# Moving the requests of three loads within a pipelined graph-attention and expert kernel

## The chip, the cores and the metric

The kernel runs on one core of one Trainium2 chip. A core has TensorE (matrix products, PE in the profile, with its weight loads as PEld), VectorE (DVE), ScalarE (ACT), GpSimd (POOL), and SyncE (SP), which here only requests transfers. Sixteen DMA engines move the data; transfers are requested by SyncE and ScalarE, or by GpSimd where rows are gathered by index. The metric is the device time of one execution in microseconds, the median of the runs.

## The reference

128 graphs of 128 nodes with 1024 features each pass through graph attention with 16 heads and then through a mixture of two of eight low-rank experts. Cut to what matters:

```python
h  = layernorm(x)                                  # x: (128 graphs, 128 nodes, 1024)
Wh = h @ W                                         # W: 1024 x 1024, 16 heads of 64
e  = leaky_relu(Wh . a1 + Wh . a2, 0.2)            # one score per node and head
att = softmax(where(adj == 0, -9e15, e)) * adj
x  = x + elu(att @ Wh)
y  = layernorm(x)
g  = softmax(top2(y[:, 0, :] @ router.T))          # a gate per graph from its first node
x  = x + (y + sum_e g_e * (y @ down_e.T) @ up_e.T) # 8 experts of rank 16, two are chosen
```

## The kernel before

The main loop takes two graphs in a step q, 64 steps and two more for the tail. The projection of two graphs is done in seven products (a Strassen-like scheme on 2 x 2 blocks: a11, a12, a21, a22 of x transposed and their sums s1 to s4). Each step has eight gaps: the tasks of gap k are issued ahead of product k+1 of that step, so each engine does its tasks in this order. The experts are handled for a group of four graphs, in a pair of steps: in the first (part 0) the router chooses two experts of each graph and GpSimd requests their weights at the end; in the second (part 1, a "fetching step") these weights arrive, the down product runs in gap 4 and the up product in gaps 5 and 6.

```python
def load_x(q):                                  # x for the sum; six buffers
    for i in (2 * q, 2 * q + 1):
        X[i] = work.tile([P, D], F32, tag="x", name="xn", bufs=6)
        nc.sync.dma_start(X[i], x[i])

def load_rows(q):                               # x for the statistics; two buffers
    for i in (2 * q, 2 * q + 1):
        ROWS[i] = work.tile([P, D], F32, tag="rows", name="rows")
        nc.sync.dma_start(ROWS[i], x[i])

def load_xt(q):                                 # x transposed, for the projection; two buffers
    XT[q] = work.tile([P, 2, KC, P], F32, tag="xt", name="xt")
    for t in range(2):
        nc.sync.dma_start(XT[q][:, t], x_t[2 * q + t])

def stats(i, mv):                               # VectorE, called by first_stats(i)
    for h in range(NH):
        nc.vector.bn_stats(st[:, h, :], ROWS[i][:, h * HALF:(h + 1) * HALF])
    nc.vector.bn_aggr(mv[:, i % 2], st)

def pair_sums(q):                               # GpSimd: s1 to s4 of the next step's projection
    nc.gpsimd.tensor_tensor(s1, a21, a22, ALU.add)
    nc.gpsimd.tensor_tensor(s2, s1, a11, ALU.subtract)
    nc.gpsimd.tensor_tensor(s3, a11, a21, ALU.subtract)     # s3 is written over a21
    nc.gpsimd.tensor_tensor(s4, a12, s2, ALU.subtract)

def turn(i):                                    # x after attention, transposed by a DMA
    nc.scalar.copy(halves, X[i].bitcast(U16).rearrange("p (d s) -> p s d", s=2))
    nc.sync.dma_start(TT[i], halves.rearrange("p s d -> p (s d)"), transpose=True)

def first_row(i):                               # SyncE; waits for update(i) on VectorE
    nc.sync.dma_start(GRP[g]["rows"][t:t + 1], X[i][0:1])

def fetch(g):                                   # end of part 0
    # ... indices on VectorE ...
    for j in range(G * TOP):                    # eight requests for the down weights
        nc.gpsimd.indirect_dma_start(out=..., in_=table, in_offset=...)
    for t in range(G):                          # four for the up weights, 512 KB each
        nc.gpsimd.indirect_dma_start(out=..., in_=up_table, in_offset=...)

def ffn_down(g):                                # pd on TensorE (64 matmuls in the profile), then
    # ... 8 chunks x 4 graphs into one accumulator pd ...
    nc.scalar.mul(whole[:, 0], pd[:, 0:P], st["gate"])              # line 845
    nc.vector.scalar_tensor_tensor(whole[:, 1], ...)                # line 846
    for t in range(G):
        for s in range(G):                      # line 850: the casts, half on each engine
            (nc.vector.tensor_copy if s // 2 else nc.scalar.copy)(
                dn[s * GR:(s + 1) * GR, t], whole[t * GR:(t + 1) * GR, s // 2])

def ffn_up(g, t):                               # pu: two accumulators a graph, from a pool of four
    for h, pu in enumerate(st["pu", t]):
        nc.tensor.matmul(pu, st["dn"][:, t], st["up", t][:, h * HALF:(h + 1) * HALF], ...)

def add_up(g, t):                               # VectorE: frees the two accumulators
    for h, pu in enumerate(st.pop(("pu", t))):
        nc.vector.scalar_tensor_tensor(y[:, cols], pu, st["rstd"][:, t:t + 1], y[:, cols], ...)
    nc.sync.dma_start(out[g * G + t], y)
```

The main loop, cut to the tasks that are spoken of:

```python
for q in range(NQ + 2):
    g, part = divmod(q - 2, 2)
    ffn = 0 <= g < NG
    # ...
    gaps[1] += [(attend, i), (update, i)]             # i = 2q - 2; first_row(i) too
    gaps[2] += [(turn, i), (update, i + 1), (squares, i)]   # and first_row(i + 1)
    gaps[3].append((turn, i + 1))
    gaps[4].append((rejoin, i))                       # ScalarE takes the transposed tile
    gaps[5].append((rejoin, i + 1))
    # ...
    if q + 1 < NQ:
        if q:
            gaps[3].append((first_stats, 2 * q + 2))
        gaps[4 if q else 5].append((pair_sums, q + 1))
        if q:
            gaps[4].append((first_stats, 2 * q + 3))
    # ...
    elif ffn and part:
        gaps[0].append((weigh, g))
        gaps[4].insert(0, (ffn_down, g))
        gaps[5][0:0] = [(ffn_up, g, 0), (ffn_up, g, 1), (add_up, g, 0), (add_up, g, 1)]
        gaps[6] += [(ffn_up, g, 2), (ffn_up, g, 3), (add_up, g, 2), (add_up, g, 3)]
    # ...
    if q + 1 < NQ:
        load_xt(q + 1)                                # ahead of all gaps of this step
        load_rows(q + 1)
    if 0 < q < NQ:
        gaps[6].insert(0, (load_x, q))
    # ...
    for gap in gaps:
        for f, *args in gap:
            f(*args)
        next(products, None)                          # the next of the seven products
```

Of the kernel before, what the change touches and what calls it, by code (L numbers as in the profile page):

```python
# [26 lines left out]
def adj_ffn_kernel(  # L27
# [32 lines left out]
    NG, _, G, _ = adj.shape  # L60
# [45 lines left out]
    def load_rows(q):  # L106
# [5 lines that stand above are left out]
    def load_xt(q):  # L112
# [3 lines that stand above are left out]
# [830 lines left out]
    def keep(name, f, *of):  # L946

        def task():
            got[name] = f(*(got.get(o, o) for o in of))
        return (task,)  # L950

    def prepare(gaps):

        gaps[0] += [(place_a,), (pair_sums, 0)]
        gaps[1] += [keep("part 0", partial_means, 0)]
        gaps[2] += [(keep_c11,), keep("part 1", partial_means, 1),
                    (center_block, 0, B11), (combine, T3, B22, T1, ALU.subtract),
                    (combine, T2, T3, B11, ALU.add)]
        gaps[3] += [(center_block, 1, B22), (combine, T1, B22, T2, ALU.subtract),
                    (sums_of, 0), keep("less", less), keep("", correct, "less", 1),  # L960
                    (load_adj, 0)]
        gaps[4] += [(score_rows, 0, 0), keep("", correct, "less", 2),
                    (center_block, 0, B21), (combine, NT4, B21, T2, ALU.subtract),
                    (sums_of, 1), (squares_of, 0), (high, 0, 0)]
        gaps[5] += [(score_rows, 0, 1), (score_rows, 1, 0), (score_rows, 1, 1), (load_experts,),
                    keep("turned", center_rows)]
        gaps[6] += [keep("", turn_rows, "turned"), (score_columns,), (low, 0, 0)]

        gaps[7] += [keep("", turn_scores, "scores")]
# [4 lines left out]
    for q in range(NQ + 2):  # L974
        gaps = [[] for _ in range(8)]
        if q == 0:
            prepare(gaps)
        g, part = divmod(q - 2, 2)
        ffn = 0 <= g < NG
        if ffn and not part:  # L980
            gaps[6] += [(logits, g), (choose, g)]
            if g < NG - 1:
                gaps[6].append((fetch, g))
        if q < NQ:
            gaps[6] += [(high, q, 3), (high, q, 1)]
            gaps[7].append((high, q, 2))
        if ffn and not part:
            gaps[6].append((ratio, g))
            if g == NG - 1:
                gaps[6].append((weigh, g))  # L990
        if 0 < q <= NQ:
            i = 2 * q - 2
            gaps[0].append((attention_weights, q - 1))
            if q > 1:
                gaps[1] += [(join, i - 2), (join, i - 1)]
            gaps[1] += [(attend, i), (update, i)]
            gaps[2].append((attend, i + 1))
            if q < NQ:
                gaps[2] += [(turn, i), (update, i + 1), (squares, i)]
                gaps[3].append((turn, i + 1))  # L1000
                gaps[4 if ffn and part else 3].append((squares, i + 1))
                gaps[5 if ffn and part else 3].append((second_stats, q - 1))
                gaps[4].append((rejoin, i))
                gaps[5].append((rejoin, i + 1))
            else:
                gaps[2] += [(squares, i), (update, i + 1), (turn_at_end, i),
                            (keep_turned, i)]
                gaps[3] += [(squares, i + 1), (turned_parts, NG - 1, False),
                            (turn_at_end, i + 1), (stay_busy, 1, ident), (turned_parts, NG - 1, True),
                            (keep_turned, i + 1), (second_stats, q - 1)]  # L1010
            if q == NQ:
                gaps[7] += [(join, i), (join, i + 1)]
            if i < B - G:
                gaps[1].append((first_row, i))
                gaps[2].append((first_row, i + 1))
        if q + 1 < NQ:
            if q:
                gaps[3].append((first_stats, 2 * q + 2))
            gaps[4 if q else 5].append((pair_sums, q + 1))
            if q:  # L1020
                gaps[4].append((first_stats, 2 * q + 3))
        if ffn and not part:
            if g < NG - 1:
                gaps[3].append((spread_rows, g))
                gaps[4].append((row_parts, g))
        if q == NQ - 1:
            gaps[1].append((load_all,))
            gaps[3].append((load_router,))
            gaps[5].append((order_all,))
        if q == NQ:  # L1030
            gaps[2].insert(1, (down_dense, NG - 1, 0, 2, range(0, 4)))
            gaps[3][0:0] = [(down_dense, NG - 1, 0, 2, range(4, 8)), (stay_busy, 2, ident)]
        if ffn and part and g == NG - 1:
            gaps[0] += [(gates_dense, g), (up_dense, g)]
# [5 lines that stand above are left out]
        if q % 2 == 0 and q < NQ:  # L1040
            gaps[5].append((group_adj, q // 2))
            if q // 2 + 1 < NG:
                gaps[5].append((load_adj, q // 2 + 1))
        if q < NQ:
            if q:
                gaps[3].insert(0, (low, q, 0))
            gaps[6 if q else 7] += [(low, q, 3), (low, q, 1)]

        if q + 1 < NQ:
            load_xt(q + 1)  # L1050
            load_rows(q + 1)
        if 0 < q < NQ:
            gaps[6].insert(0, (load_x, q))
        if q == 0:
            gaps[7] += [(sums_of, 2), (sums_of, 3), (load_up,)]
        if q == 1:
            gaps[0].append((squares_of, 1))
            gaps[1].append((up_parts,))
            gaps[5] += [keep("tables", table_parts), keep("router", router_sums)]
            gaps[7].append(keep("", experts, "tables", "router"))  # L1060
        products = project(q) if q < NQ else iter(())
# [3 lines that stand above are left out]
            next(products, None)  # L1065
# [46 lines left out]
```

## Time and profile before

| What | Before |
|---|---|
| time, median of 3 runs (lowest to highest) | 1982.6 us (1980.53 to 1983.49) |
| span of the profiled execution | 1980.3 us |
| granted TensorE clock, mean | 0.997 |
| mean rate of all DMA | 226 GB/s, 446.87 MB |
| SyncE's queue (q1) | 353.70 MB, 58.9% of the DMA engines' time |
| GpSimd's queue (q0) | 89.68 MB, 14.5% |
| xt, x for statistics, x for the sum | 127, 126 and 128 requests of 512 KB |
| gathered down and up weights | 248 and 124 requests |

A row of a waits view reads "who waited <- for what: us in total, times, longest us". "issue" means that the profile shows nothing that was waited for. A row of a timeline reads: start in us, duration in us, engine, line, operation, output<-inputs, and how many instructions; in brackets the idle time ahead of it and what ended it. Ends of matmuls are modelled, so the distance from one start to the next start tells more than a duration. A row of a windows view holds the stretch, its length, the busy us and the number of instructions on TensorE, its weight loads, VectorE, ScalarE and GpSimd, and then the granted clock, the DMA engines' mean busy share and GB/s. Names: pw is the accumulator of the projection, ph of the attention, pd of the down product, pu of the up product; xn is x for the sum, rows is x for the statistics (and, with 4 KB, the first rows), tt is a tile transposed by DMA.

### The profile page before, as it was taken

How to read it: one execution, taken by the hardware profiler on the slowest of the kernel's cores; microseconds unless marked ns; L12 is line 12 of the kernel's file. 1: busy time of each engine (PE TensorE's matmuls, PEld its weight loads, DVE VectorE, ACT ScalarE, POOL GpSimd, SP SyncE). 2: the span in 40 equal slices, each digit the busy share in tenths (PEclk: the TensorE clock that was granted, in tenths of full speed). 3: DMA queues.
4: the chain of work that ended last, by engine and by line, in shares of the span. 5: the costliest groups of instructions: out<-in, count | busy, mean ns of one | idle time of the engine just before them, and what ended most of it. 6: DMA issues, size and time to landing. Idle time of an engine off the chain costs nothing.

```text
span 1980.3 us, 30167 instructions
## 1 busy us (share of the span) xinstructions
PE 1907.6 (96%) x10182; PEld 1590.9 (80%) x10182; DVE 1689.8 (85%) x3802; ACT 1294.6 (65%) x1564; POOL 944.1 (48%) x1260
## 2 busy tenths in 40 slices
PE   9999999999999999999999999999999999999997
PEld 6878887788888788888888888888888888777885
DVE  6888898888898888888888988888888889888897
ACT  3766666766577666667666676676676666665665
POOL 3346544455444455444555444554444654436541
PEclk9999999999999999999999999999999999999999
DMA  8688767877777767677777777777778676778755
GB/s 323 185 236 200 242 216 224 238 221 213 246 236 202 255 209 237 219 229 235 243 206 241 225 220 240 211 226 236 235 212 255 200 245 218 220 240 204 231 186 166
DMA packets 381058, 446.87 MB, mean 226 GB/s; under 512 B 282732, under 2 KB 284908, under 8 KB 380392
## 3 DMA queue, kind: packets, MB, share of 16 engines
q1 hardware_dynamic: 345320, 353.70, 58.9%
q0 software_dynamic: 30400, 89.68, 14.5%
q10 hardware_dynamic: 5184, 1.57, 0.3%
q8 instruction: 81, 1.33, 0.3%
q14 instruction: 73, 0.60, 0.1%
HBM read 309.58 MB, written 69.22 MB: 191 GB/s over the span
## 4 chain that ended last, share of the span: by engine, by line
PE 86%; DVE 5%; issue 3%; DMA 3%; POOL 2%; ACT 1%; another core or an unknown queue 0%; SPq 0%; DVEq 0%; ACTq 0%
PE pw L480 73%; PE ph L594 5%; PE pd L836 4%; PE pu L858 3%; DMA up<-up_table,at_up 2%; POOL down L820 1%; DVE xn L867 1%; DMA w_sb<-in_w 1%; DVE wh L485 1%; POOL up L826 0%; DVE parts L550 0%; PE pu L922 0%; DVE hp L604 0%; DVE xn L618 0%
## 5 line engine op out<-in xcount | busy, mean ns | idle before, releaser
L480 PE MATMUL pw<-w_sb,xt 128*128 128x260 f32 (+1 forms) x4080 | 935.5, 385 | 0.5 <-DMA w_sb<-in_w 0.5
L480 PEld LDWEIGHTS pw<-w_sb,xt 128*128 128x128 f32 x4080 | 771.7, 190 | 125.5 <-issue 7.0
L480 PE MATMUL pw<-w_sb,s 128*128 128x260 f32 (+1 forms) x3072 | 704.9, 382 | 0.6 <-DVE wh L485 0.6
L480 PEld LDWEIGHTS pw<-w_sb,s 128*128 128x128 f32 x3072 | 582.8, 190 | 95.7 <-DVE wh L485 2.3
L664 ACT COPY y_t<-tt 128x2048 uint16<-128x2048 uint16 x126 | 310.4, 2492 | 54.5 <-DMA tt<-halves 54.3
L638 POOL TENSOR_SCALAR rstd<-acc 128x2 f32<-128x2 f32 x64 | 12.3, 193 | 693.9 <-ACT unread L626 681.6
L658 ACT COPY halves<-xn 128x2048 uint16<-128x2048 uint16 x126 | 239.9, 1904 | 88.5 <-DVE xn L618 73.1
L820 POOL DMA_INDIRECT down<-table,at_down x248 | 260.5, 1050 | 77.8 <-issue 65.8
L546 ACT ACTIVATE parts<-wh,rstd 128x512 fp32r<-128x512 f32 x192 | 136.9, 719 | 227.9 <-DVE wh L485 227.9
L604 DVE TENSOR_TENSOR hp<-ph,att 128x512 f32<-128x512 f32 x256 | 166.0, 684 | 25.9 <-remote 10.2
L618 DVE SCALAR_TENSOR_TENSOR xn<-ex,xn 128x1024 f32<-128x1024 f32 x128 | 156.8, 1225 | 34.7 <-ACT ex L611 24.6
L611 ACT ACTIVATE ex<-hp 128x1024 f32<-128x1024 f32 x128 | 135.1, 1055 | 69.9 <-DVE hp L604 43.5
L867 DVE SCALAR_TENSOR_TENSOR xn<-pu,rstd,xn 128x512 f32<-128x512 f32 x248 | 168.5, 741 | 1.0 <-PE pu L858 1.0
L594 PE MATMUL ph<-parts,adj_f 128*128 128x512 f32 x512 | 164.7, 443 | 1.7 <-ACT parts L546 0.9
L485 DVE TENSOR_TENSOR wh<-pw,p 128x520 f32<-128x520 f32 (+1 forms) x192 | 131.7, 686 | 35.8 <-PE pw L480 20.4
L612 DVE SCALAR_TENSOR_TENSOR xn<-hp,xn 128x1024 f32<-128x1024 f32 x128 | 156.8, 1225 | 4.4
L377 DVE BATCH_NORM_STATS2 stats<-rows 128x6 f32<-128x512 f32 x248 | 158.6, 681 | 0.4
L826 POOL DMA_INDIRECT up<-up_table,at_up x124 | 135.1, 1089 | 37.8 <-issue 37.2
L684 ACT ACTIVATE xn<-xn,off,mul 128x1024 f32<-128x1024 f32 x128 | 151.8, 1235 | 0.0
L626 ACT ACTIVATE unread<-xn,acc 128x1024 fp8e4<-128x1024 f32 x126 | 143.9, 1142 | 3.3 <-DVE acc L620 2.5
L550 DVE SCALAR_TENSOR_TENSOR parts<-wh,rstd,parts 128x512 fp32r<-128x512 f32 x192 | 137.7, 743 | 6.9 <-ACT parts L546 6.8
L836 PE MATMUL pd<-y_t,down 128*32 128x128 f32 x1984 | 84.2, 277 | 42.0 <-issue 41.9
(187 smaller groups left out, 1890.1 us busy)
## 6 DMA issues: line engine op xcount, KB each, us to landing
xn<-in_x SPq DMA_DIRECT2D x128, 512.0 KB
xt<-in_x_t SPq DMA_DIRECT2D x127, 512.0 KB
rows<-in_x SPq DMA_DIRECT2D x126, 512.0 KB
out_y<-xn SPq DMA_DIRECT2D x124, 512.0 KB
adj_f<-in_adj_t POOLq DMA_DIRECT2D x32, 256.0 KB
adj_i<-in_adj SPq DMA_DIRECT2D x32, 256.0 KB
down<-table,at_down POOLq DMA_INDIRECT x248
w_sb<-in_w SPq DMA_DIRECT2D x3, 1040.0 KB
```

Of the source, the lines that this page charges most:

```text
L377: nc.vector.bn_stats(st[:, h, :], ROWS[i][:, h * HALF:(h + 1) * HALF])
L480: nc.tensor.matmul(dst[:, j, cols], lhs[:, k, :], w_sb[:, rhs, k, j, cols], start=(first and k == 0), stop=(k == KH - 1), skip_group_check ...
L594: nc.tensor.matmul(PH[i][h], GRP[g]["adj_f"][:, t, :], PARTS[q][:, s, NH * (i % 2) + h], start=(s == 0), stop=(s == 1))
L604: nc.vector.tensor_tensor(hp[:, h * HALF:(h + 1) * HALF].rearrange("p (h f) -> p h f", f=F), ph.rearrange("p (h f) -> p h f", f=F), att[:, ...
L612: nc.vector.scalar_tensor_tensor(xt, hp, 0.0, xt, op0=ALU.max, op1=ALU.add)
L618: nc.vector.scalar_tensor_tensor(xt, ex, 1.0, xt, op0=ALU.min, op1=ALU.add, accum_out=acc[:, 0])
L658: nc.scalar.copy(halves, X[i].bitcast(U16).rearrange("p (d s) -> p s d", s=2))
L664: nc.scalar.copy(y_of(i).bitcast(U16).rearrange("p k (n s) -> p s k n", s=2), TT.pop(i).rearrange("p (s k) n -> p s k n", s=2))
L684: nc.scalar.activation(X[i], X[i], AF.Identity, bias=GRP[g]["off"][:, t:t + 1], scale=GRP[g]["mul"][:, t:t + 1])
L820: nc.gpsimd.indirect_dma_start(out=st["down"][:, j * R:(j + 1) * R].rearrange("p r k -> p (r k)"), out_offset=None, in_=table, in_offset=b ...
L836: nc.tensor.matmul(pd[t * GR:(t + 1) * GR, 0:P], st["down"][:, t * GR:(t + 1) * GR, k], st["y_t"][:, k, t * P:(t + 1) * P], start=(k == 0) ...
L867: nc.vector.scalar_tensor_tensor(y[:, cols], pu, st["rstd"][:, t:t + 1], y[:, cols], op0=ALU.mult, op1=ALU.add)
```

## The change

In a fetching step, xt and x for statistics of the next step are requested at the head of gap 3 and no longer at the step's start, and what uses them moves too: the two first statistics go from gaps 3 and 4 to gaps 4 and 5, and the pair sums from the end of gap 4 to gap 5, behind the first two graphs of the up product. In the other steps x for the sum is requested at the head of gap 3 and no longer of gap 6. It is meant to keep the time in which the chosen experts' weights are gathered free of other large loads. No operation is added or taken away.

```diff
--- before.py
+++ after.py
@@ -977,6 +977,7 @@
             prepare(gaps)
         g, part = divmod(q - 2, 2)
         ffn = 0 <= g < NG
+        fetching = ffn and part and g < NG - 1
         if ffn and not part:
             gaps[6] += [(logits, g), (choose, g)]
             if g < NG - 1:
@@ -1014,11 +1015,14 @@
                 gaps[1].append((first_row, i))
                 gaps[2].append((first_row, i + 1))
         if q + 1 < NQ:
+
+            late = int(fetching)
             if q:
-                gaps[3].append((first_stats, 2 * q + 2))
-            gaps[4 if q else 5].append((pair_sums, q + 1))
+                gaps[3 + late].append((first_stats, 2 * q + 2))
+            at = gaps[4 + late if q else 5]
+            at.insert(0 if late else len(at), (pair_sums, q + 1))
             if q:
-                gaps[4].append((first_stats, 2 * q + 3))
+                gaps[4 + late].append((first_stats, 2 * q + 3))
         if ffn and not part:
             if g < NG - 1:
                 gaps[3].append((spread_rows, g))
@@ -1047,10 +1051,9 @@
             gaps[6 if q else 7] += [(low, q, 3), (low, q, 1)]
 
         if q + 1 < NQ:
-            load_xt(q + 1)
-            load_rows(q + 1)
+            gaps[3 if fetching else 0][0:0] = [(load_xt, q + 1), (load_rows, q + 1)]
         if 0 < q < NQ:
-            gaps[6].insert(0, (load_x, q))
+            gaps[6 if fetching else 3].insert(0, (load_x, q))
         if q == 0:
             gaps[7] += [(sums_of, 2), (sums_of, 3), (load_up,)]
         if q == 1:
```

## The prediction

> **What bounds the kernel now.** I read the page first (busy shares, then the chain that ended last), then TensorE's waits, then the timeline of one weight-fetching step on all engines, then DMA activity in short windows.
>
> ```profile
> PE 1907.6 (96%) x10182; PEld 1590.9 (80%) x10182; DVE 1689.8 (85%) x3802; ACT 1294.6 (65%) x1564; POOL 944.1 (48%) x1260
> PE pw L480 73%; PE ph L594 5%; PE pd L836 4%; PE pu L858 3%; DMA up<-up_table,at_up 2%; POOL down L820 1%; DVE xn L867 1%; DMA w_sb<-in_w 1%; DVE wh L485 1%; POOL up L826 0%; DVE parts L550 0%; PE pu L922 0%; DVE hp L604 0%; DVE xn L618 0%
> ```
>
> TensorE is the bound: 1907.6 of 1980.3 us, and 73% of the chain is the projection itself. The change removes no matmul, so only idle or slowed TensorE time can be won. TensorE's waits say where that is:
>
> ```profile
> PE pd L836 <- issue: 41.9, 57, 1.9
> PE pu L858 <- DMA up<-up_table,at_up: 6.3, 3, 3.2
> PE pu L858 <- issue: 5.2, 25, 0.2
> ```
>
> All of it lies in the 31 steps that fetch weights: the down product (pd) and the up product (pu). Everything else on TensorE between two such steps is rigid: from the last pu of one to the first pd of the next I read 46.1 us in 26 of the 30 intervals. A usual fetching step in TensorE's timeline:
>
> ```profile
> 1324.82 0.44 PE L836 MATMUL pd<-y_t,down 128*32 128x128 f32 x4
> 1326.30 0.38 PE L836 MATMUL pd<-y_t,down 128*32 128x128 f32 x2 [1.03 <-issue]
> 1327.02 1.91 PE L836 MATMUL pd<-y_t,down 128*32 128x128 f32 x58 [0.34 <-issue]
> 1328.86 3.77 PE L480 MATMUL pw<-w_sb,xt 128*128 128x260 f32 x16
> 1332.63 1.18 PE L858 MATMUL pu<-up,dn 128*128 128x512 f32 x4
> 1333.65 3.67 PE L480 MATMUL pw<-w_sb,s 128*128 128x260 f32 x16
> 1336.97 0.98 PE L858 MATMUL pu<-up,dn 128*128 128x512 f32 x2
> 1338.15 1.11 PE L858 MATMUL pu<-up,dn 128*128 128x512 f32 x2 [0.21 <-issue]
> ```
>
> Two losses are to be seen, by starts. (a) pd takes 1328.86-1324.82 = 4.04 us with 1.03+0.34 us idle. (b) The second four pu take 1339.10 (the next product's start) -1336.97 = 2.13 us where the first four took 1.02: 1.11 us lost. Loss (b) is VectorE's doing; the weight loads of pu wait 20.8 us in 55 waits for its additions (xn, line 867):
>
> ```profile
> 1330.62 0.34 DVE L846 SCALAR_TENSOR_TENSOR dn<-pd,gate,dn 128x128 fp32r<-128x128 f32 x1
> 1330.99 2.98 DVE L850 CAST dn<-dn 32x128 fp32r<-32x128 f32 x8
> 1333.98 1.29 DVE L377 BATCH_NORM_STATS2 stats<-rows 128x6 f32<-128x512 f32 x2
> 1335.31 0.21 DVE L378 BATCH_NORM_AGGREGATE mv<-stats 128x2 f32<-128x12 f32 x1
> 1335.43 0.65 DVE L485 TENSOR_TENSOR wh<-pw,wh 128x520 f32<-128x520 f32 x1
> 1335.99 2.71 DVE L867 SCALAR_TENSOR_TENSOR xn<-pu,rstd,xn 128x512 f32<-128x512 f32 x4
> ```
>
> The additions that free the accumulators start at 1335.99 although their products ended near 1333.8; casts and statistics stand ahead of them. The eight casts take 2.98 us where eight medians of 222 ns make 1.8: one is held up to 1.3 us. Last, the DMA share and GB/s over this step:
>
> ```profile
> 1309.00:1317.00 8.00, 8.00 (x38) 6.87 (x37) 7.43 (x26) 4.24 (x6) 6.02 (x7) 1.00 0.88 334
> 1317.00:1322.00 5.00, 5.00 (x24) 4.29 (x23) 3.83 (x7) 2.45 (x2) 3.93 (x4) 1.00 0.29 68
> 1326.00:1331.00 5.00, 4.36 (x70) 3.68 (x70) 2.98 (x7) 3.75 (x8) 3.60 (x3) 1.00 0.79 295
> 1334.00:1338.00 4.00, 3.94 (x18) 2.91 (x16) 3.96 (x8) 4.00 (x2) 2.06 (x6) 1.00 0.00 0
> ```
>
> xt and x for statistics run in the first window, the gathered down weights trickle in the second, the up weights run in the third, and in the last nothing runs.
>
> **What the Trainium skill says.** "SBUF — State Buffer" lets VectorE casts in a two-port mode and GpSimd exclude each other for a whole instruction. The trace agrees: the long cast lies under GpSimd's pair sums (1.26 to 1.32 us each, 1327.32 to 1332.45). "DMA: Bandwidth & Descriptors", section "Queues, rings and completion order", says that one ring's descriptors start in order and that each DMA engine alternates between rings packet by packet, so xt on the sync queue and up weights on GpSimd's should share. No step before has large loads on both for long, so the even share below is an estimate. Section "Specifications" gives 435 GB/s as ceiling; full windows here show 406 to 418.
>
> **The change part by part.** Nothing is added or removed; three things move.
>
> 1. In 30 or 31 steps, four requests (xt twice, x for statistics twice, 512 KB each, 2.1 MB) leave the step's start (1309.07) for the head of gap 3. On the sync queue that is behind the request of the first rows at 1324.88: not three products but 16 us later, since that request waits for VectorE. Issue is 0.4 us each: 1325.1 to 1327. What this frees is the window 1309 to 1317. What was there with it is the gathered down weights, but their eight requests are paced by GpSimd (1.3 us each, the last 1318.83 to 1319.86), after that window. So I expect no earlier last down weight. The pd idle ends within 0.3 us of 7.0 us after GpSimd's last down request in all 31 steps, also in the last one, which has no xt to load (0.86 us idle against 1.35 on average). I book pd at 0 to -0.3 us per step, i.e. about -5 us in all.
>
> 2. The new load: transposed halves hold the sync queue until about 1325.5, and the time from request to first bytes in the step's start is about 1.7 us (requested 1309.07, traffic from 1310.8). So xt starts near 1327, when up weights still have some 1.2 MB to come (they end at 1330 at about 400 GB/s). Shared evenly at 205 GB/s each, up ends about 5.9 us later, 1332.9, before its last use at 1338. In that time 1.2 MB of mine are in: xt (1.05 MB, done near 1332.1) and 0.15 MB of the first x. The other 0.37 MB at 410 GB/s take 0.9 us: the first x is there near 1333.8, the second near 1335. The turned second tile follows and ends near 1338 where it ended at 1334; ScalarE takes it 1.7 us later than the 1336 of before, and the attention which needs that chain is at 1346.
>
> 3. VectorE in gaps 4 and 5. The first statistics move from before pd's casts to behind them, the second from before the additions of graphs 0 and 1 to behind them. With the pair sums now waiting for xt (1332), the casts run free in 1.8 us. New order: casts 1330.4 to 1332.3; statistics when x is there, t_r; 1.5 us of statistics, 0.6 us for the projection's sum, additions from t_r+2.0. Before: 1335.99. So t_r below 1334.0 is a gain and above it a loss, one for one on TensorE; the gain stops at the 1.1 us of loss (b). My t_r, with 0.2 us of landing, is 1334.0: break-even. Per us of error: 31 us over the kernel.
>
> 4. In about four of the 31 steps the second transpose is requested early, runs mixed with the up weights and makes both crawl; pu then waits 0.6 to 3.2 us (the 6.3 us row) and intervals after two of them are 1.5 us longer. Now 2 MB of xt and x stand between in the same ring, so I book -8 us.
>
> 5. x for the sum comes three gaps sooner in the other steps. Its buffers were freed a step earlier, so no wait; it delays the second transpose there by about 1 MB / 410 = 2.5 us of traffic less the idle it fills, perhaps 1 us, which ScalarE's later waits (0.9 and 1.9 us) absorb. 0 us.
>
> Sum: -5 (pd) + 0 (additions) - 8 (early transposes) + 5 for waits on late x that come unevenly = -8: 1982.6 - 8, about 1975.
>
> **The rivals.** *Full relief:* up weights yield to the sync queue, x is there by 1332.9, additions start 1.1 us sooner: 31 x 1.1 = 34, with the 13 above 1935 to 1940. For it: 4 us of idle DMA after 1334 show room; against: the up weights fill the queue to 1330. *Late x:* transposes are slow when mixed with other traffic (fetching step at 1808 us: pu waited for up until 1823.57), so x comes 1.5 us later, VectorE blocks in gap 4 with the additions behind it: +46, about 2025. For it: everything is now pushed into 1322 to 1335. *The fetch really was in the way:* the pd idle is caused by xt's traffic and goes: -42, about 1940. Against: it ends 7 us after the last request even where no xt was loaded.
>
> **Range and chances.** t_r has an error of about 1.2 us either way, so about 35 us, capped on the good side by 1.1 us. Range 1940 to 2012. Over 2% faster (below 1943) needs full relief or the pd idle gone: 0.12. Over 2% slower (above 2022) needs x over 1.4 us late: 0.10. Within: 0.78.
>
> **What would show it.** Right: pd idle near 40 us still on the page, casts of dn on VectorE at 222 ns with no long one, the second statistics behind four additions, the wait for up weights gone, DMA busy in the former empty 1334 to 1338. Wrong: VectorE's statistics waiting for rows for more than 2 us per step (late x), pd idle falling by more than half, the second four pu at 1.1 us (full relief), or the interval of 46.1 us growing.

## The result, and the profile after

The changed kernel takes 2074.3 us (median of 4 runs, 2070.9 to 2083.4) where the kernel before takes 1982.3 us (4 runs): a ratio of 1.047 with a 95% interval of 1.043 to 1.051. It is slower by 92 us. Predicted were 1975 us, in a range of 1940 to 2012.

The two lines of the page that answer to those of before, the busy time of each engine and the chain that ended last by line:

```profile
PE 1957.8 (95%) x10182; PEld 1621.7 (78%) x10182; DVE 1645.4 (80%) x3802; ACT 1299.2 (63%) x1564; POOL 941.4 (45%) x1260
DMA rows<-in_x 13%; PE pw L480 8%; DMA first_row<-rows 6%; DVE wh L485 5%; DVE hp L604 5%; DVE xn L618 5%; DVE parts L550 5%; DVE xn L867 5%; DVE xn L612 4%; SPq L660 4%; DMA out_y<-xn 3%; DMA rows<-xn 2%; ACT ex L611 2%; DVE stats L377 2%; DVE prod L713 1%
```

The same 10182 matmuls keep TensorE busy 50 us longer, which points to a lower clock (0.981 on the mean against 0.997), and the chain has left TensorE: it was 73% projection before and is now x for statistics (13%), first rows (6%) and VectorE. The view of all waits names the same two loads. Neither load's row was of any size before (none for x; first rows 0.6 us, once):

```profile
ACT y_t L664 <- DMA tt<-halves: 158.5, 62, 5.1
...
DVE stats L377 <- DMA rows<-in_x: 96.5, 30, 5.3
...
PE pd L836 <- issue: 50.3, 102, 1.3
DVE prod L713 <- DMA first_row<-rows: 45.4, 31, 3.7
...
PE pu L858 <- issue: 34.8, 50, 2.7
```

The down product's idle went from 41.9 to 50.3 us, the up product's "issue" wait from 5.2 to 34.8, and its 6.3 us of waiting for up weights are gone. The fetching step that the prediction showed at 1324.82 lies at 1387.54 here. TensorE's timeline of it:

```profile
1387.54 0.54 PE L836 MATMUL pd<-y_t,down 128*32 128x128 f32 x5
1388.65 0.32 PE L836 MATMUL pd<-y_t,down 128*32 128x128 f32 x1 [0.57 <-issue]
1389.37 0.27 PE L836 MATMUL pd<-y_t,down 128*32 128x128 f32 x1 [0.39 <-issue]
1390.09 1.80 PE L836 MATMUL pd<-y_t,down 128*32 128x128 f32 x57 [0.46 <-issue]
1391.86 3.75 PE L480 MATMUL pw<-w_sb,xt 128*128 128x260 f32 x16
1395.25 1.28 PE L858 MATMUL pu<-up,dn 128*128 128x512 f32 x4
1396.37 3.67 PE L480 MATMUL pw<-w_sb,s 128*128 128x260 f32 x16
1400.95 1.11 PE L858 MATMUL pu<-up,dn 128*128 128x512 f32 x2 [0.91 <-issue]
```

pd now takes 4.32 us from its start to the next product's start (4.04 before), and the second four pu start 4.58 us after their product instead of 3.32. The requests on the sync queue and VectorE's work in this step say why:

```profile
1384.11 3.50 SPq L660 DMA_TRANSPOSE tt<-halves  x1
1387.71 0.38 SPq L692 DMA_DIRECT2D rows<-xn  x1
1388.19 0.84 SPq L115 DMA_DIRECT2D xt<-in_x_t  x2
1389.08 1.28 SPq L110 DMA_DIRECT2D rows<-in_x  x2
```

```profile
1393.47 1.89 DVE L850 CAST dn<-dn 32x128 fp32r<-32x128 f32 x8
1398.10 1.29 DVE L377 BATCH_NORM_STATS2 stats<-rows 128x6 f32<-128x512 f32 x2 [2.74 <-DMA rows<-in_x]
1399.42 0.21 DVE L378 BATCH_NORM_AGGREGATE mv<-stats 128x2 f32<-128x12 f32 x1
1399.54 0.65 DVE L485 TENSOR_TENSOR wh<-pw,wh 128x520 f32<-128x520 f32 x1
1400.10 2.72 DVE L867 SCALAR_TENSOR_TENSOR xn<-pu,rstd,xn 128x512 f32<-128x512 f32 x4
```

The casts run free in 1.9 us, VectorE is ready for the statistics at 1395.4, and x lands only at 1398.1. The additions that free pu's accumulators stand behind it and TensorE waits for them.

**Where the 92 us are.** I cut each of the 30 periods between two down products at starts in TensorE's timeline and took means, in us. The projection's products bear the kernel's own numbers: "product 7" is the one between pd and pu, "product 3" the one between the two halves of pu; "rest" is everything from the last pu to the next pd.

| kernel | pd | product 7 | first four pu | product 3 | second four pu | rest | period |
|---|---|---|---|---|---|---|---|
| before | 4.01 | 3.66 | 1.03 | 3.31 | 2.32 | 46.26 | 60.59 |
| after | 5.09 | 3.56 | 1.12 | 4.61 | 2.30 | 46.80 | 63.49 |

The period grew by 2.90 us, which over 31 is 90 of the 92 us: pd 1.08, product 3 with the wait behind it 1.30, the rest 0.54. Most of the last is a matter of the clock. In the 10 of the 30 intervals that hold a stretch at half clock the rest takes 47.7 us, in the other 20 46.35. A windows view of the stretch after pu's wait in the step above (columns as in the prediction: length, busy times, then clock, DMA share, GB/s) shows what makes the 10:

```profile
1399.90:1403.30 3.40, 2.00 (x6) 0.94 (x6) 3.40 (x6) 1.89 (x1) 3.14 (x5) 1.00 0.55 174
1403.30:1406.70 3.40, 3.40 (x11) 2.67 (x10) 3.37 (x7) 1.92 (x3) 1.41 (x5) 0.56 0.77 283
1406.70:1410.00 3.30, 3.30 (x16) 2.83 (x15) 3.20 (x9) 0.58 (x1) 0.00 (x0) 0.94 0.50 128
```

After a stretch with 1.4 us of idle TensorE, 3.4 us follow at about half clock, in which 11 matmuls pass instead of 16. The down product has the same: in 20 steps it took 4.73 us to its last matmul's end (4.08 before), in the other 10, whose matmuls took some 417 ns where 273 is usual, 5.96. Over the whole run the mean clock is 0.981 against 0.997: (1-0.981) x 2069 - (1-0.997) x 1980 = 39.3 - 5.9 = 33 us of full-speed TensorE time, at most, were lost to the clock alone.

### The profile page after: what moved, and what is told of

Same layout as the page of the kernel before. It is cut to its first block, busy times and chain, and to the rows that moved or that the text cites. A ratio compares the mean times of both kernels' runs of the same rounds, so it can differ in the third digit from the quotient of the medians.

```text
span 2069.1 us, 30197 instructions
## 1 busy us (share of the span) xinstructions
PE 1957.8 (95%) x10182; PEld 1621.7 (78%) x10182; DVE 1645.4 (80%) x3802; ACT 1299.2 (63%) x1564; POOL 941.4 (45%) x1260
## 4 chain that ended last, share of the span: by engine, by line
DVE 47%; DMA 25%; PE 9%; issue 7%; ACT 6%; SPq 5%; DVEq 0%; another core or an unknown queue 0%; ACTq 0%; POOL 0%; POOLq 0%
DMA rows<-in_x 13%; PE pw L480 8%; DMA first_row<-rows 6%; DVE wh L485 5%; DVE hp L604 5%; DVE xn L618 5%; DVE parts L550 5%; DVE xn L867 5%; DVE xn L612 4%; SPq L660 4%; DMA out_y<-xn 3%; DMA rows<-xn 2%; ACT ex L611 2%; DVE stats L377 2%; DVE prod L713 1%
## 5 line engine op out<-in xcount | busy, mean ns | idle before, releaser
L480 PE MATMUL pw<-w_sb,xt 128*128 128x260 f32 (+1 forms) x4080 | 950.4, 389 | 2.1 <-issue 0.9
L480 PEld LDWEIGHTS pw<-w_sb,xt 128*128 128x128 f32 x4080 | 783.7, 194 | 134.6 <-issue 11.5
L664 ACT COPY y_t<-tt 128x2048 uint16<-128x2048 uint16 x126 | 314.9, 2500 | 158.7 <-DMA tt<-halves 158.5
L377 DVE BATCH_NORM_STATS2 stats<-rows 128x6 f32<-128x512 f32 x248 | 158.6, 681 | 96.5 <-DMA rows<-in_x 96.5
L430 POOL TENSOR_TENSOR s<-xt 128x512 f32<-128x512 f32 x64 | 81.5, 1273 | 272.9 <-DMA xt<-in_x_t 177.1
L836 PE MATMUL pd<-y_t,down 128*32 128x128 f32 x1984 | 108.2, 314 | 50.3 <-issue 50.3
L550 DVE SCALAR_TENSOR_TENSOR parts<-pw,rstd,parts 128x512 fp32r<-128x512 f32 x63 | 47.3, 751 | 123.2 <-ACT sc L506 123.2
```

The lines of the kernel that those rows point to most:

```text
L480: nc.tensor.matmul(dst[:, j, cols], lhs[:, k, :], w_sb[:, rhs, k, j, cols], start=(first and k == 0), stop=(k == KH - 1), skip_group_check ...
L664: nc.scalar.copy(y_of(i).bitcast(U16).rearrange("p k (n s) -> p s k n", s=2), TT.pop(i).rearrange("p (s k) n -> p s k n", s=2))
```

## The experiments

The expectations speak of two theories. **A**: there are two separate waits. x for the sum, requested in gap 3 of the other steps, stands on the DMA engines ahead of the 16 KB read of the first rows, so the experts are chosen later, the down weights are requested later, and pd is longer; and in the fetching steps x for statistics lands late and VectorE's additions stand behind it. **B**: the second wait makes the whole loss, and x for the sum is innocent. Runs were spread over three chips. On the first the kernel before takes 1981 us; on the second and third it takes 1931 and 1933 us. Which chip before and after above ran on isn't on record; in their time (1982 us) and in pd's idle they are like the first. Each ratio is against the kernel before on the same chip, and times are compared only within a chip.

### 1. Only x for the sum moves

```diff
 (before)
-            gaps[6].insert(0, (load_x, q))
+            gaps[6 if fetching else 3].insert(0, (load_x, q))
```

> The kernel before, with only x for the sum requested three gaps sooner in the steps that fetch nothing. Theory A (two separate waits): 1 MB of x now stands ahead of the small read of the first rows, VectorE's router product waits for it about 1.5 us, the gather requests come 0.9 us later, and since the down product's idle ends 7 us after the last down request, that product grows from 4.0 to about 5.0 us in each of 31 steps: +30 us, 2012 us, ratio 1.015. Theory B (all of the loss comes from the late xt and x, and load_x is innocent): ratio 1.000 to 1.003, the read of the first rows waited for as little as before.

2006.4 us against 1981.3, ratio 1.013 (1.010 to 1.015). Its waits view has the row of first rows and no row for x:

```profile
PE pd L836 <- issue: 50.2, 75, 2.1
DVE prod L713 <- DMA first_row<-rows: 50.0, 31, 3.3
```

A holds for this part, and B, which had 1.000 to 1.003, falls. The down weights' first request came 14.85 us before pd's start instead of 15.30, and pd took 5.15 us. The table's way of reading adds something that A left out: in 17 of the 30 steps pd ended only 0.49 us later than before, in 13 it ran at the lower clock and ended 1.97 us later. The second four pu gave 0.71 us of it back (1.61 instead of 2.32), because a later pd lets VectorE come free. The mean clock is 0.986; (1-0.986) x 2005 - 5.9 = 22 us, about as much as the whole loss. That the ratio came so near to A's 1.015 is partly luck: the requests moved by half of the 0.9 us that A had, and the clock made up for it.

### 2. Only the fetching steps' part

```diff
 (after)
-            gaps[6 if fetching else 3].insert(0, (load_x, q))
+            gaps[6].insert(0, (load_x, q))
```

> The changed kernel with x for the sum requested in gap 6 everywhere, so only xt, x for statistics and their users come late. Theory A: the down product is back at 4.0 us, the stretch before the second four up products stays at 4.6 us instead of 3.3: about 2035 us, ratio 1.027. Theory B: as slow as the changed kernel, ratio 1.04 to 1.05.

2050.3 us, ratio 1.034 (1.032 to 1.036). Now the waits view has x and hardly any first rows:

```profile
DVE stats L377 <- DMA rows<-in_x: 114.8, 30, 5.7
...
PE pu L858 <- issue: 48.8, 59, 3.2
PE pd L836 <- issue: 38.8, 69, 1.7
...
DVE prod L713 <- DMA first_row<-rows: 2.0, 5, 0.7
```

pd is back at 4.03 us and product 3 takes 5.09. The additions start 12.90 us after pd's start, 1.87 us later than the 11.03 of before, and product 3 is 1.78 us longer: one for one. The ratio lies between A's 1.027 and B's 1.04: pd is what A said, and the late x costs more than A gave it. The two parts apart cost 25 and 69 us, which makes 94 where the whole change costs 92, so nothing else of size is in the change. They do overlap: with both, the longer pd hides 0.48 us of the late x (product 3 4.61 us against 5.09 here).

### 3. Only VectorE's order

Loads at the step's start as before, but statistics and pair sums in the changed gaps, so that nothing waits for x:

```diff
 (experiment 2)
-            gaps[3 if fetching else 0][0:0] = [(load_xt, q + 1), (load_rows, q + 1)]
+            load_xt(q + 1)
+            load_rows(q + 1)
```

> The kernel before with only the order of the users changed in the fetching steps (statistics and pair sums a gap later), all loads requested where they were. If the order is good and only the landing of x is bad: casts on VectorE in 1.8 us, additions over 1 us sooner, the second four up products in 1.1 us instead of 2.1: 31 x 1.0 to 1.1, about 1950 us, ratio 0.984. If the order itself costs (the second statistics now stand before the projection's sum of gap 5 and before the second four additions): the stretch before the second up products grows over 3.3 us and the ratio is 1.00 or above.

2014.8 us, ratio 1.017 (1.015 to 1.019), a miss: the gain didn't come, and the loss isn't where the other branch put it, since product 3 stays at 3.31 us. VectorE's and GpSimd's timelines of one step:

```profile
1341.79 3.55 DVE L850 CAST dn<-dn 32x128 fp32r<-32x128 f32 x8
1345.35 1.29 DVE L377 BATCH_NORM_STATS2 stats<-rows 128x6 f32<-128x512 f32 x2
```

```profile
1341.32 1.27 POOL L433 TENSOR_TENSOR xt<-xt 128x512 f32<-128x512 f32 x1
1342.55 1.27 POOL L434 TENSOR_TENSOR s<-xt,s 128x512 f32<-128x512 f32 x1
```

With xt present early, GpSimd takes the pair sums early, whatever gap they stand in, and they lie under the casts, which take 3.56 us a step where after has 1.77. So the casts' gain comes from xt being late, not from the order of instructions. The additions start no sooner (11.12 against 11.03 us). Its six runs spread from 1995.7 to 2022.5 us, the two fastest at a clock of 0.994 and 0.996, the others at 0.987 to 0.990; the profiled run is one of the two, so where the rest of this loss lies isn't shown.

### 4. x for statistics ahead, xt behind

```diff
 (experiment 2)
-            gaps[3 if fetching else 0][0:0] = [(load_xt, q + 1), (load_rows, q + 1)]
+            gaps[3 if fetching else 0][0:0] = [(load_rows, q + 1), (load_xt, q + 1)]
```

> As e2, but in the late requests x for statistics stands ahead of xt. If VectorE's wait for x is what counts: x lands about 3 to 5 us sooner, the wait of the statistics goes from 3 us per step to under 1, the stretch before the second up products returns to about 3.3: 35 us less than e2, about 2000 us. If late xt (the pair sums on GpSimd and with them the next projection) is what counts: no better than e2, or worse, since xt then lands later still.

1988.6 us, ratio 1.0035 (1.0025 to 1.0045): 62 us below experiment 2 (35 were expected), for an exchange of two requests in one queue. Waits:

```profile
POOL s L430 <- DMA xt<-in_x_t: 264.0, 23, 12.7
...
DVE stats L377 <- DMA rows<-in_x: 5.4, 5, 3.0
```

GpSimd waits for xt longer than in any other run on this chip, and the whole kernel is only 7 us slower than before; VectorE's wait for x is gone, and product 3 is back at 3.34 us. The loss of the fetching steps is VectorE's wait for x, not late loads as such.

### 5. After, with x for the sum one gap later

```diff
 (after)
-            gaps[6 if fetching else 3].insert(0, (load_x, q))
+            gaps[6 if fetching else 4].insert(0, (load_x, q))
```

> The changed kernel with x for the sum in the steps that fetch nothing one gap later, at the head of gap 4, where its request stands behind the second transpose and the read of the first rows is already out. Theory A: the read lands before the 1 MB, VectorE's wait for it (45 us) is nearly gone, the down product falls from 5.1 to about 4.1 us: like e2, 2050 us, ratio 1.033. If it was not the place ahead of that read but the earlier load as such that disturbs the fetch, it stays at 1.045.

2087.6 us on the second chip, ratio 1.083 (1.078 to 1.088). The number expected was for a chip on which pd idles, and this one has no such idle: pd takes 1.92 us in one piece. So the run didn't answer its question; it was put again in experiment 10. It showed something else: with pd 2 us shorter, x is no sooner there (11.18 us after pd's start), the wait for x grows to 193.5 us and product 3 to 7.27 us.

### 6. Only xt late

```diff
 (experiment 3)
-            load_xt(q + 1)
+            gaps[3 if fetching else 0].insert(0, (load_xt, q + 1))
             load_rows(q + 1)
```

x for statistics is requested at the step's start as before; statistics and pair sums stand in the changed gaps.

> e3 with xt alone requested at gap 3; x for statistics at the step's start; statistics and pair sums a gap later. GpSimd's pair sums then wait for xt and leave VectorE's casts alone (1.8 us a step, in e3 3.6), and x is there in time: additions from about 9.5 us after the down product's start instead of 11.1, the second four up products in 1.1 us instead of 2.3 to 2.5: about 1955 us, ratio 0.985. If late xt itself costs (transposed tile behind it, later attention): ratio 1.00 or above, with the rest of the two steps over 46.3 us.

1915.2 us against 1930.6, ratio 0.993 (0.990 to 0.996). VectorE's casts are down to 1.78 us a step, VectorE waits for no load of any size (1.7 us in all, for first rows), and the second four pu take 1.22 us. The gain is half of the expected one, and the first four pu take 1.98 us. The kernel before has no trace on this chip, so it isn't shown which stretch the 15 us come from.

### 7. Half of the up weights' gathers left out

```diff
 (before)
+                if t > 1:
+                    st["up", t] = st["up", t - 2]
+                    continue
```

This leaves out the gathers of the up weights of graphs 3 and 4 of each group; those graphs multiply with the weights of graphs 1 and 2.

> The kernel before, but it leaves out the gathers of up weights for the third and fourth graph of a group and takes those of the first two there, so its time is not that of the whole work. The down product's idle ends 7.0 us after the last request for down weights in every run so far, 1.2 to 1.5 us after the last for up weights. If the up gathers behind it hold the release: with two fewer (2.5 us of requests) the idle ends about 4.5 us after the last down request, that is ahead of the product, and the product takes 2.2 us instead of 4.0. If it is a fixed delay of the down gathers: still 7.0 us and 4.0 us.

1904.4 us, ratio 0.987 (0.983 to 0.990). It was to tell whether the up requests on GpSimd hold back pd's release. It ran on the chip without pd's idle (pd 2.02 us), so it tells nothing on that.

### 8 and 11. xt late, both statistics where they were

```diff
 (before)
-            gaps[4 if q else 5].append((pair_sums, q + 1))
+            at = gaps[4 + int(fetching) if q else 5]
+            at.insert(0 if fetching else len(at), (pair_sums, q + 1))
...
-            load_xt(q + 1)
+            gaps[3 if fetching else 0].insert(0, (load_xt, q + 1))
```

> The kernel before with only xt requested at gap 3 and the pair sums in gap 5 of the fetching steps; x for statistics and both statistics stay where they were. Casts on VectorE 1.8 us instead of 3.0, first statistics in the time in which VectorE is idle anyway, additions from about 9.6 us after the down product's start instead of 11.0, second four up products in about 1.1 us instead of 2.3: 31 x 1.1 less, about 1948 us, ratio 0.983; as e6 or a little better. If late xt itself costs: 1.00 or above.

> e8 again. On a chip where the down product idles 1.4 us a step: casts 1.8 us, second four up products in 1.1 to 1.3 us, ratio 0.983 to 0.990. On a chip without: 0.992 again.

The same kernel on the second and the third chip: 1916.2 us against 1930.6, ratio 0.992 (0.990 to 0.994), and 1917.9 against 1933.3, ratio 0.992 (0.989 to 0.995). It is 0.8% faster than the kernel before on both chips, again half of what was expected at first, and 189 us faster than the changed kernel, run on the third in experiment 9. TensorE's timeline of a step on the second chip:

```profile
1286.57 1.98 PE L836 MATMUL pd<-y_t,down 128*32 128x128 f32 x64
1288.48 3.77 PE L480 MATMUL pw<-w_sb,xt 128*128 128x260 f32 x16
1291.90 0.82 PE L858 MATMUL pu<-up,dn 128*128 128x512 f32 x2
1294.06 0.70 PE L858 MATMUL pu<-up,dn 128*128 128x512 f32 x2 [1.33 <-DVE xn L867]
1294.60 3.67 PE L480 MATMUL pw<-w_sb,s 128*128 128x260 f32 x16
1297.91 1.28 PE L858 MATMUL pu<-up,dn 128*128 128x512 f32 x4
1299.03 2.13 PE L480 MATMUL pw<-w_sb,xt 128*128 128x260 f32 x9
```

pd's 64 matmuls run without a gap, and the second four pu take the 1.1 us that the prediction hoped for; the first four have a wait of their own now (1.98 us on the mean). Late xt keeps GpSimd's pair sums off VectorE's casts (1.77 us), while x is there long before it is needed. It wasn't run on the first chip.

### 9, 10 and 12 on the third chip

Experiment 9 is the changed kernel unaltered. Experiment 10 is experiment 5 again. Experiment 12 is experiment 8 with xt requested at the end of gap 4, behind the second transpose:

```diff
 (experiment 8)
-            gaps[3 if fetching else 0].insert(0, (load_xt, q + 1))
+            if fetching: gaps[4].append((load_xt, q + 1))
+            else: gaps[0].insert(0, (load_xt, q + 1))
```

> The changed kernel unaltered, to stand on the same chip as the next three; e5 ran on a chip where the kernel before takes 1931 us and the down product never idles. If that chip is met again: like e5 about 1.08, since x lands as late and there is no idle in the down product to hide it. If a chip like the first is met: 1.045 again.

> As e5, now beside the changed kernel. Where the down product idles: 25 to 35 us less than e9, the down product back near 4.1 us. Where it doesn't idle: the gather requests come 0.6 us sooner than in e9 and the time is within 1% of e9, since nothing waits for the gathered weights there.

> e8 with xt requested one gap later still, behind the second transpose. The up weights and that transpose then have the DMA engines alone: the wait of the first four up products for up weights (e8: 20.5 us, 1.98 us instead of 1.1 a step) is gone, 20 us less than e8, ratio 0.980 to 0.985. If xt then lands too late for the pair sums (needed some 22 us after the down product's start): the projection of the next step waits and it is slower than e8.

The changed kernel takes 2107.1 us here, ratio 1.090 (1.086 to 1.093), so the change costs 174 us where pd doesn't idle and 92 where it does. Waits, and one step on TensorE:

```profile
DVE stats L377 <- DMA rows<-in_x: 207.9, 30, 10.4
PE pu L858 <- issue: 124.8, 31, 5.4
DVE prod L713 <- DMA first_row<-rows: 34.5, 31, 2.0
```

```profile
1415.41 1.98 PE L836 MATMUL pd<-y_t,down 128*32 128x128 f32 x64
...
1421.86 3.67 PE L480 MATMUL pw<-w_sb,s 128*128 128x260 f32 x16
1428.84 2.73 PE L858 MATMUL pu<-up,dn 128*128 128x512 f32 x4 [3.31 <-issue]
```

The first statistics start 11.66 us after pd's start, on the first chip 11.51: x is equally late, but pd ends 3.2 us sooner, and product 3 is longer by that (7.87 us against 4.61). The mean clock is 0.953, worth up to (1-0.953) x 2107 - (1-0.997) x 1933 = 99 - 6 = 93 us of the 174.

Experiment 10 took 2088.1 us, ratio 1.080 (1.077 to 1.084): 19 us less than experiment 9. The first rows' wait is gone, the down weights' first request comes 15.26 us ahead of pd instead of 14.96, and the loss through x stays. 19 us are within the 1% expected, but not for the reason given: nothing waits for down weights here, and product 3 (7.39 us against 7.87) holds 15 of the 19.

Experiment 12 took 2059.1 us, ratio 1.065 (1.061 to 1.070), a miss. No load of x or xt is late for VectorE, yet:

```profile
PE pu L858 <- DMA up<-up_table,at_up: 114.9, 24, 6.3
DVE xn L867 <- PE pu L858: 94.5, 22, 5.5
```

In the step I read the second transpose was requested at 1378.21, and the up weights it mixed with held pu until 1390.33, 3.5 us of idle. In experiment 8 the first of these rows has 20.5 us. The transpose isn't requested any sooner here (1.69 us after pd's start on the mean, 1.62 in experiment 8), but there 1 MB of xt stands ahead of it in the same queue. By the packets of the trace the DMA engines move some 150 GB/s from 7 to 11 us after pd's start here, 270 in experiment 8. So the loads of xt in gap 3 look like a spacer between the two; that is read from these traces, and late xt, for which GpSimd waits 305.6 us here, wasn't parted from it by a run.

## Why the prediction was wrong

**Step 5, "0 us" for x for the sum, failed first.** It looked only at the second transpose, whose delay ScalarE absorbs, and not at the small read next in line. The first rows' 16 KB are read back in gap 3 of the same steps, on ScalarE's queue but over the same DMA engines; behind the 1 MB of x at that gap's head the read takes 4.0 us from issue to landing (median), and VectorE waits 45 us for it in 31 steps; with x one gap later that wait is gone (experiments 5 and 10). VectorE's product of them moreover slips under GpSimd's pair sums, 1034 ns instead of 407. Choosing and gathering begin 0.6 us later. Experiment 1 prices the part at 25 us; a lower clock in 13 of 30 down products is most of that.

**Step 1's rule held, and turned against the step.** pd's idle ended 7.04 us after the last down request before and 7.11 us after it now, 6.9 to 7.1 in experiments 1 to 4. "No earlier last down weight" was right: without xt and x in the way (experiment 2) pd takes 4.03 us. But the step took the time of the last request itself as fixed. It came 0.55 us later, pd ended 0.65 us later in 20 steps, and in 10 it ran at the lower clock besides: (20 x 0.65 + 10 x 1.88) / 30 = 1.06 us a step, +33 us where -5 stood.

**Step 2's t_r failed.** It put the first x 9.2 us after pd's start; the mean is 11.5. The last of the four requests ended 3.24 us after pd's start and not 2.2, since a transpose holds the queue first (3.50 us of issue in the step above). That isn't the main error: in experiment 2 it ended at 2.07 us, as predicted, and the statistics still began at 10.89. The packets of after's trace, as means over the steps, say more. The even share held: from 5 to 7 us after pd's start the up weights move at 196 GB/s and the sync queue at 214. 2.2 us after pd's start the up weights had 1.46 MB to come and not 1.2, and by the count of the sync queue's bytes xt and one x were through at 9.9 us where 9.0 was worked out. The statistics began 1.6 us after that where 0.2 us of landing were booked, close to the 11.3 us at which the bytes of all four requests were through. Why the first x is complete so late wasn't tested by a run.

**Step 3 was right in its mechanism, and its break-even exact.** The casts run in 1.77 us, the additions start 2.01 us after the first statistics where t_r + 2.0 was said, and TensorE pays one for one: the additions are 2.49 us later, pd's own delay of 1.08 takes up part, and product 3 pays 1.30. The second four pu kept their loss (2.30 us). With t_r at 11.5 the step's own rule gives (2.49 - 1.08) x 31 = 44 us; 40 came.

**Step 4 was right in kind.** The wait for up weights is gone, 6.3 us. But the "intervals 1.5 us longer" which it counted as the transposes' doing each hold a stretch at half clock, as the 10 long ones of after do behind a wait of another kind (47.7 against 46.35 us). So -8 was too much: the rest of the period grew by 17 us.

**No step had the clock.** "TensorE: Matmul & The Clock Gate" of the Trainium skill, section "Part 1: The HAM clock gate", says that TensorE falls to half clock after an idle window of some 3.4 us and returns to full clock after a busy one. The trace agrees on the half and on the length: 0.56 in the 3.4 us shown above, full clock on either side. It differs on what sets it off: here 1.4 us of idle in such a stretch were followed by it (the skill has a whole idle window). Idle length alone doesn't decide either: pd before had single waits up to 1.9 us and no drop in any of 30 steps, pd after none above 1.3 and a drop in 10. The traces' clock records show what goes with it. In every one of the fourteen traces the stretches at half clock begin on one grid of 3.413 us, to within 4 ns. In after, 38 intervals of this grid have TensorE busy for at most 66% of the time; 22 of them are followed by half clock, all 9 below 48% among them, and no interval above 66% is. In before there are 16 such intervals, and only the 3 below 40% are followed by it. So where a pause falls on the grid and how much else of the interval is idle count besides its length; between 48% and 66% these figures don't decide.

The sum: +33 (pd), +40 (product 3), +17 (rest, clock) and about 0 for the others make 90 us. Of the rivals *late x* was the right one; its 46 us (1982.6 + 46 is 2029, not 2025) came from x 1.5 us late, and x was 2.3 us late. That a mixed-in transpose makes it late, as the rival had it, isn't shown. Two of the prediction's own signs of being wrong came: VectorE waits 3.2 us a step for rows (96.5 us in 30), and the interval of 46.1 us grew. Its chance was set by an error of 1.2 us in t_r, half of what it was, and the range fell short through that, through step 5 and through the clock.

What stays open is what holds pd's release for 7 us after the last request on the first chip and not on the other two. Experiment 7 was to tell and ran on a chip without it.

## What to carry to other kernels

When a large load moves, list every small read that shares the DMA engines with it and leads to a decision: here 16 KB behind 1 MB cost 25 us, lower clock included, though nothing waited for the 1 MB itself. Before loads are bunched behind a transpose on one queue, ask which of them an in-order engine takes first, and put that one first; the exchange of two requests was worth 62 us here, and the engine that could wait did so for 264 us in a kernel only 7 us slower than before. Price a new stall on TensorE with the lower clock after it, not by its length alone.

## What the hardware showed unexpectedly

- Small stalls drew a lower clock after them. That the stall brings it on was read from the records, in after and in experiment 1, and not tested by a run of its own. Experiment 1 delays the down requests by 0.45 us and its 25 us stand beside some 22 us of full-speed time lost to a mean clock of 0.986.
- The same kernel took 1981, 1931 and 1933 us on three chips. The down product goes with it: 4.0 to 5.2 us in the traces of the first, 1.9 to 2.0 in those of the other two. But the kernel before has no trace on those two, and 2.1 us in 31 steps would make 65 us where 48 to 50 are seen, so that this is the whole cause isn't shown. The change costs 174 us on the third and not 92, since a shorter pd hides less of the late x and the clock drops further.
- VectorE's casts took 217 to 225 ns each where no pair sum of GpSimd ran beside them (after), and up to 1348 ns where one did (experiment 3), which agrees with the Trainium skill, "SBUF — State Buffer", section "SBUF: two separate sides", where a shared pair of ports goes to one of the two for a whole instruction; experiment 3 shows that moving instructions in GpSimd's list doesn't part the two, as long as the data are there.
- A transpose that runs while gathered weights still arrive seems to hold them back: 114.9 us of waits for up weights in experiment 12, 20.5 in experiment 8, for requests of xt moved by one gap.
